# A timetable for two graph layers: in the pair attention, features are stored ahead of the pair's weights, the second layer's parts stand closer, and score rows are loaded later

## The chip, the core and the metric

The kernel runs on one core of a Trainium2 chip. The metric is the device time of one execution in microseconds. Before the change the median of three runs is 3165.02 us (3162.23 to 3175.48); the profiled execution has a span of 3169.2 us, and all times below that name a moment count from its start.

## The reference

The input is 128 graphs of 128 nodes with 256 features and a 128x128 adjacency each. Two layers follow each other. Cut to what matters:

```python
# layer 0
for W, a in ((W1, a1), (W2, a2)):             # two graph attentions
    Wh = h @ W
    e = leaky_relu(Wh @ a[:F] + swap(Wh @ a[F:]), 0.2)
    h = softmax(where(adj > 0, e, NEG), axis=1) @ Wh
h = layernorm(x + h)
x1 = layernorm(h + relu(h @ w_ff1) @ w_ff2)   # "ff0"
# layer 1: attention of 8 heads with a value matrix per relation
attn = softmax(q @ k / sqrt(32))
out = sum_r (attn * (adj == r)) @ v_r
x2 = layernorm(x1 + out @ Wo)                 # "att"
y = layernorm(x2 + gelu(x2 @ W1) @ W2)        # "ff1"
```

All of it is float32.

## The kernel before, in words

**Tiles and stages.** Four graphs make a group (`G = 4`), so there are 32 groups. Each group goes through five stages, each a Python generator: `load` (the transposed input `xt` and the adjacency `at`), `gat` (both graph attentions, `gat_block`, L428), `ff0` (the first feed forward), `att` (the attention of the second layer, `attention`, L460) and `ff1` (the second feed forward, `feed_forward`, L315). When the adjacency has no entry above 1, as here, the arm with the plan `BINARY` runs. It takes the attention of a group by pairs of graphs (`together=2`): scores of a pair (`weights`, L482), their transposition (`turned`, L511), the masks (`by_relation`), the weighted sum (`weighted`, matmuls at L557 into the tile `av`) and the output product (L584). Below, "#1" is the first pair of a group and "#2" the second.

**What sets the order.** Each `yield TIMES[...]` in a stage gives a number of units to pass before the stage goes on. In `layers` (L603) a heap holds the next moment of every stage of every group; a stage of group g starts at `period * g + begin[stage] - early`, with a period of 100 units. The work that a stage emits between two yields thus gets a place in one list, and this list is binding for two engines: for SP, the queue that issues all transfers, over the whole of the list, and for PE, the matmul engine, from moment 280 on (`kept={PE: 280, SP: 0}`):

```python
t, n, g, steps = heapq.heappop(todo)
step = next(steps, None)                  # emits the work up to the next yield
...
    if e in last and kept[e][0] <= t <= kept[e][1]:
        tc.add_manual_dep(i, last[e], ...)   # order of emission
if step is not None:
    heapq.heappush(todo, [t + step, n, g, steps])
```

The units are an order and no times. The order on DVE, ACT and POOL is chosen by the framework's scheduler, as are the PSUM banks: `mm` has 7 (`bufs`), and `av` one of its own. Five groups are in flight at a time, each in another stage.

**Transposition through memory.** A product needs its token tile with features on the partitions. `put` (L267) transposes 32x32 blocks on DVE (L282) and stores four quarters to a DRAM buffer `zd` (four stores, L285); after `yield TIMES["put"]`, `get` loads the whole back (L291). This serves `ff0`, `att` and `ff1` (tile `T`, by `features`, L296) and the attention weights of each graph (`e1` stored, `eT` loaded). `turned` stores both graphs of a pair (eight stores), waits `put`, loads the first, waits `next put`, loads the second.

**The score rows of a graph attention.** `gat_weighting` (L394) stores one row per graph to `zsd` (L405), waits `row put`, loads it to all partitions as `e` (L408), waits `row`, and then adds the column term (ACT, L411), takes the leaky maximum, the mask and the row maximum (DVE, L418 to L420), the exponential (ACT, L423), the reciprocal (L424) and the scaling (POOL, L425). After `gat` units the product with `wh` follows: L444 for the first graph attention, L455 for the second.

**The feed forward.** After `moving_sums` (POOL, L309 to L312) come eight visits, which alternate between two units of hidden features; each visit emits products at L333 and copies, sums and activations on ACT, DVE and POOL (L339 to L360). The third and fourth products of a unit write a bank that ACT copies out first (L346, L351). Then the second matrix (L378): a first half of 32 matmuls over the first unit's features, and a second half in two parts of 8 ("k0" and "k2"), each of which ends in an addition on DVE (L388).

**The pair attention.** Its list is: `features` (put, get), mask load (L242), q and k (L470, L475), scores #1 (L491), `turned` #1, values #1 (L542), masks #1 (L526), weighted sum #1 with scores #2 right behind it, output product #1 (L584, after `wo` units), `turned` #2, values #2, masks #2, weighted sum #2, output product #2. A pair's scores take four of the seven `mm` banks; each is read by a maximum on DVE (L495) and by four exponentials on ACT (L504), 16 for a pair.

Of the kernel before, what the change touches and what calls it, by code (L numbers as in the profile page):

```python
# [29 lines left out]
TIMES = {  # L30
    "sums": 5, "ff visits": (2.5, 2.5, 3, 3, 3.25, 3.25, 3.25, 3.25), "ff2": 3,
    "ff first half": 10, "ff half": 5, "row": 13, "gat": 22, "wh": 5.5,
    "gat copy": 2, "qk": 7, "scores": 18, "mask": 7, "av": 13, "wo": 8, "turned": 10,
    "put": 7, "next put": 3, "row put": 5,
    "lead ff0": 19, "lead att": 25, "lead ff1": 25, "affine": 7,
    "store": 25,
}
# [3 lines left out]
    binary=False, times=TIMES, together=1, period=560, bufs=dict(T=3, tok=2, m=4, mm=6, v=1),  # L41
    begin=dict(load=-97, gat=-61, ff0=48, att=132, ff1=400), early={},
# [1 line left out]
)  # L44

BINARY = dict(
    binary=True, times=TIMES, together=2,
    period=100, bufs=dict(T=5, tok=5, m=2, mm=7, v=2),
    begin=dict(load=-97, gat=-61, ff0=48, att=132, ff1=300),
    early={  # L50
        (1, "ff0"): 48,
        (2, "load"): 80, (2, "gat"): 80, (2, "ff0"): 80,
        (3, "load"): 5,
        (-2, "ff1"): -15,
        (-1, "load"): 5,
    },
    kept={PE: 280, SP: 0},
)
# [726 lines left out]
```

## Time and profile before

| what | value |
|---|---|
| median of three runs | 3165.02 us |
| span of the profiled execution | 3169.2 us |
| PE busy | 2816.0 us (89%) |
| ACT, POOL, DVE busy | 1682.8, 1529.4, 1510.3 us |
| mean share of the DMA engines (queue q1) | 47.3% |
| starts of L455 of one group: fourth and thirty-second | 260.39 and 2917.09 us |

A group's L455 stands at the same place of each period, so the distance of two of them is the length of a period: (2917.09 - 260.39) / 28 = 94.9 us. Idle time of an engine is put down to what released it. "SPq" is SP's queue, in which a transfer and its waits hold up all that stands behind them. PE's granted clock, in the windows view, is 1.00 at full speed.

### The profile page before, as it was taken

Reading aid. Unit: us, or ns where it says so; the run is one execution under the profiler, and the core shown is the slowest. Engines: PE = TensorE matmul, PEld = TensorE weight load, DVE = VectorE, ACT = ScalarE, POOL = GpSimd, SP = SyncE. Lnnn points to the kernel's source line nnn. Section 1 sums busy time; section 2 is a strip of 40 time slices with the busy share of each in tenths; the row PEclk is TensorE's granted clock in tenths of the full one; section 3 lists DMA queues with packets and bytes.
Section 4 is the critical chain, followed back from the end, with each engine's and each line's share of the span. In section 5 each row is a group of like instructions: output and inputs, shape, how many; then the busy total and the mean of one; then the engine's idle time right before and its main releaser. Section 6 shows DMA issues by size and latency. Waiting matters only on the chain.

```text
span 3169.2 us, 46779 instructions
## 1 busy us (share of the span) xinstructions
PE 2816.0 (89%) x16578; PEld 2173.5 (69%) x16578; DVE 1510.3 (48%) x2873; ACT 1682.8 (53%) x5063; POOL 1529.4 (48%) x1610
## 2 busy tenths in 40 slices
PE   4988989889889889889889889889889889889878
PEld 3756677667677667667667677667677667677656
DVE  5454455445445444455445445444455444445342
ACT  2455465555465554565555565555565555565443
POOL 1434455454455454555354455453555454555362
PEclk6998999999999999999999999999999999999999
DMA  6145554544543644554544553544654544543420
GB/s 262 41 90 121 122 107 89 124 88 102 125 105 90 126 97 90 127 110 90 121 91 98 125 109 86 127 98 89 127 110 86 124 89 98 127 104 80 90 50 14
DMA packets 1156947, 328.76 MB, mean 104 GB/s; under 512 B 903008, under 2 KB 1126752, under 8 KB 1156064
## 3 DMA queue, kind: packets, MB, share of 16 engines
q1 hardware_dynamic: 1156704, 325.68, 47.3%
q8 instruction: 133, 2.18, 0.3%
q14 instruction: 110, 0.90, 0.1%
HBM read 195.97 MB, written 129.62 MB: 103 GB/s over the span
## 4 chain that ended last, share of the span: by engine, by line
PE 34%; ACT 21%; POOL 18%; issue 11%; DMA 7%; SPq 5%; DVE 3%; ACTq 0%; POOLq 0%; DVEq 0%
PE mm L378 14%; ACT e L504 7%; POOL tok L265 6%; PE mm L470 5%; DMA T<-zd 5%; SPq L285 5%; POOL e L507 4%; ACT fT L354 4%; POOL rstd L256 4%; ACT tok L259 4%; PE mm L333 3%; PE mm L475 3%; PE av L557 3%; PE mm L542 3%; ACT e L423 1%
## 5 line engine op out<-in xcount | busy, mean ns | idle before, releaser
L265 POOL TENSOR_TENSOR tok<-tok,ln_rows 128x512 f32<-128x512 f32 x476 | 618.5, 1320 | 20.8 <-PE mm L276 12.8
L378 PE MATMUL mm<-w,fT 128*128 128x256 f32 x2048 | 460.7, 381 | 0.0
L378 PE MATMUL mm<-wf,fT 128*128 128x256 f32 x2048 | 456.7, 381 | 1.5 <-ACT fT L354 1.5
L378 PEld LDWEIGHTS mm<-w,fT 128*128 128x128 f32 x2048 | 386.6, 190 | 67.4 <-issue 13.9
L378 PEld LDWEIGHTS mm<-wf,fT 128*128 128x128 f32 x2048 | 386.4, 190 | 57.5 <-ACT fT L354 1.9
L507 POOL TENSOR_TENSOR e<-e,s 128x1024 f32<-128x1024 f32 x128 | 241.4, 1897 | 343.2 <-DVE s L506 269.0
L504 ACT ACTIVATE e<-mm,nm 128x128 f32<-128x128 f32 x1024 | 358.2, 394 | 46.2 <-DVE nm L495 45.8
L259 ACT ACTIVATE tok<-tok,nmr,rstd 128x256 f32<-128x256 f32 x480 | 249.1, 589 | 200.7 <-POOL nmr L257 189.3
L309 POOL TENSOR_TENSOR t<-T 128x256 f32<-128x256 f32 x64 | 50.8, 793 | 550.1 <-DMA T<-zd 550.1
L470 PE MATMUL mm<-T,wq 128*128 128x512 f32 x256 | 183.2, 881 | 137.3 <-DMA T<-zd 137.3
L425 POOL TENSOR_TENSOR e<-e,s 128x512 f32<-128x512 f32 (+1 forms) x68 | 68.1, 1002 | 430.4 <-DVE s L424 393.6
L526 DVE TENSOR_TENSOR m<-eT,am 128x1024 f32<-128x1024 f32 x128 | 176.8, 1397 | 184.0 <-DMA eT<-zd 183.5
L495 DVE TENSOR_REDUCE nm<-mm 128x4 f32<-128x512 f32 x256 | 162.3, 680 | 200.8 <-PE mm L491 200.8
L352 POOL TENSOR_TENSOR fT<-fT 128x512 f32<-128x512 f32 x128 | 161.3, 1271 | 178.3 <-ACT fT L351 178.3
L542 PE MATMUL mm<-wv,T 128*128 128x512 f32 x512 | 240.7, 615 | 0.0
L504 ACT ACTIVATION_READ_ACCUMULATOR e<-mm,nm 128x1 f32 x1024 | 240.3, 235 | 0.0
L470 PEld LDWEIGHTS mm<-T,wq 128*128 128x128 f32 x256 | 70.8, 289 | 233.9 <-DMA T<-zd 144.3
L476 ACT ACTIVATE kT<-mm,col 128x512 f32<-128x512 f32 x64 | 43.9, 687 | 326.4 <-PE mm L475 326.4
L333 PE MATMUL mm<-T,w 128*128 128x256 f32 x768 | 196.3, 384 | 0.7 <-ACT T L280 0.2
L333 PE MATMUL mm<-T,wf 128*128 128x256 f32 x768 | 192.8, 381 | 0.0
L561 ACT COPY oT<-av 128x512 f32<-128x512 f32 x64 | 37.4, 585 | 276.9 <-PE av L557 276.9
L360 ACT ACTIVATE fT<-mm,col 128x256 f32<-128x256 f32 x256 | 107.2, 472 | 137.8 <-PE mm L333 97.8
(142 smaller groups left out, 5371.6 us busy)
## 6 DMA issues: line engine op xcount, KB each, us to landing
zd<-e SPq DMA_DIRECT2D x496, 128.0 KB, 3.5
eT<-zd SPq DMA_DIRECT2D x124, 512.0 KB, 6.2
zd<-T SPq DMA_DIRECT2D x364, 128.0 KB, 3.5
T<-zd SPq DMA_DIRECT2D x91, 512.0 KB, 4.3
xt<-in_xT_dram SPq DMA_DIRECT2D x32, 512.0 KB, 5.6
e<-zsd SPq DMA_DIRECT2D x60, 256.0 KB, 4.1
tok<-in_x_dram SPq DMA_DIRECT2D x30, 512.0 KB, 4.9
out_dram<-tok SPq DMA_DIRECT2D x29, 512.0 KB, 6.0
```

The costliest lines, as they stand in the source:

```text
L259: nc.scalar.activation(y[:, b], y[:, b], AF.Identity, bias=nmr[:, b:b + 1], scale=rstd[:, b:b + 1])
L265: engine.tensor_tensor(y[:, b:b + n], y[:, b:b + n], v[:, None, :].to_broadcast([P, n, D]), op)
L285: nc.sync.dma_start(s[:, :, i].rearrange("k (j a) t -> a (k j) t", a=Q), z[ts(i, Q)].rearrange("a k (j t) -> a (k j) t", t=Q))
L333: nc.tensor.matmul(p[:, i], win[k][:, ts(f0 + i, P)], hs[k], start=first and i == 0, stop=True, skip_group_check=True)
L352: nc.gpsimd.tensor_add(hi[:, :, 1], hi[:, :, 1], hi[:, :, 0])
L378: nc.tensor.matmul(ys[b // 2][:, b % 2], fT[f][:, ts(b, N)], wout[:, f], start=b % 2 == 0 and n == 0, stop=n == FC - 1, skip_group_check=True)
L470: nc.tensor.matmul(p, c.wq[:, f, ts(i, P)], hT[:, :, f], start=f == 0, stop=f == DC - 1)
L495: nc.vector.tensor_reduce(nm.rearrange("p j i -> p (j i)"), p.rearrange("p j i n -> p (j i) n"), AX.X, OP.max, negate=True)
L504: nc.scalar.activation(e[:, k], p[:, j, i], AF.Exp, bias=nms[q][:, j, i:i + 1], accum_out=s[:, k:k + 1])
L507: nc.gpsimd.tensor_mul(e, e, per_row(s, N))
L526: nc.vector.tensor_tensor(m, eT, at[:, b][:, None, :].to_broadcast([P, H, N]), OP.mult)
L542: nc.tensor.matmul(p, hT[:, b, f], wv[:, f, r:r + 2], start=f == 0, stop=f == DC - 1)
```

## The change

Only numbers of the plan `BINARY` change. It gets times of its own for twelve of the yields, and other starts for four stages.

```diff
-    binary=True, times=TIMES, together=2,
-    period=100, bufs=dict(T=5, tok=5, m=2, mm=7, v=2),
-    begin=dict(load=-97, gat=-61, ff0=48, att=132, ff1=300),
+    binary=True, together=2, period=100, bufs=dict(T=5, tok=5, m=2, mm=7, v=2),
+    times=dict(TIMES, **{
+        "ff first half": 6, "ff half": 4, "row": 14.5, "wh": 3.5, "mask": 8.5, "av": 14.5,
+        "wo": 12, "turned": 11, "next put": 2.5, "row put": 9, "affine": 9,
+        "ff visits": (2.5, 2.5, 4, 4, 3.25, 3.25, 3.25, 3.25),
+    }),
+    begin=dict(load=-96, gat=-61, ff0=45, att=129, ff1=303),
     early={
-        (1, "ff0"): 48,
+        (1, 'ff0'): 46,
```

Before, the same entries are: ff first half 10, ff half 5, row 13, wh 5.5, mask 7, av 13, wo 8, turned 10, next put 3, row put 5, affine 7, and ff visits (2.5, 2.5, 3, 3, 3.25 four times). The other lines of `early` change their quotes only. No instruction is added or removed in a period; what changes is where the instructions stand on each engine and which bank or buffer each tile gets. What it is for: the attention's features are to be stored and loaded ahead of the weights of the pair before, the parts of the second feed-forward matrix are to stand closer together, and the score rows are to be loaded 9 units after they are stored, so that each engine finds its operands ready.

In one period (moments modulo 100) the two binding lists read, with "get" for L291 and "put" for L285:

```
SP before: att put 32, e1 #2 put 37, att get 39, eT #2 get 44 and 47, ff0 put 48, zsd 50, e 55, ff0 get 55
SP after:  att put 29, att get 36, e1 #2 put 41.5, ff0 put 45, zsd 46, eT #2 get 48.5 and 51, ff0 get 52, e 55

SP before: e1 #1 put 89, zsd 92, eT get 96, e 97, eT get 99, ff1 put 0, load 3, ff1 get 7
SP after:  e1 #1 put 86, eT get 93, zsd 93.5, eT get 95.5, e 2.5, ff1 put 3, load 4, ff1 get 10

PE before: ff0 first half 6, k0 16, av #1 + scores #2 19, k2 21, wo #1 27, L455 32, ff1 visits from 37, L436 39 and 44.5, values #2 47, ff1's last visit 57.75, q k 64, ff1 first half 64, av #2 67, scores #1 71, k0 74, wo #2 75, ff0 visits from 79, k2 79, L444 90, values #1 99
PE after:  ff0 first half 5, k0 11, k2 15, av #1 + scores #2 18.5, wo #1 30.5, L455 39, L436 39 and 42.5, ff1 visits from 40, values #2 51, q k 61, ff1's last visit 62.75, scores #1 68, ff1 first half 69, av #2 74, k0 75, ff0 visits from 76, k2 79, wo #2 86, L444 91.5, values #1 95.5
```

More of the change, by code (lines that the diff above doesn't have):

```diff
@@ L46 @@
 BINARY = dict(
-    binary=True, times=TIMES, together=2,
-    period=100, bufs=dict(T=5, tok=5, m=2, mm=7, v=2),
-    begin=dict(load=-97, gat=-61, ff0=48, att=132, ff1=300),
-    early={
-        (1, "ff0"): 48,
[L52 to L55, printed above, removed]
+    binary=True, together=2, period=100, bufs=dict(T=5, tok=5, m=2, mm=7, v=2),
[5 more added lines that the diff above has]
+    begin=dict(load=-96, gat=-61, ff0=45, att=129, ff1=303),
+    early={
+        (1, 'ff0'): 46,
+        (2, 'load'): 80,
+        (2, 'gat'): 80,
+        (2, 'ff0'): 80,
+        (3, 'load'): 5,
+        (-2, 'ff1'): -15,
+        (-1, 'load'): 5,
     },
```

## The prediction

> **What bounds the kernel now.** I read the page first, then PE's waits, the timeline of one period for PE, SP and ACT, and the windows view for the clock. The page says that PE carries the span (89% busy, the next engine 53%), so time is won only where PE idles or runs slowly.
>
> ```profile
> PE 2816.0 (89%) x16578; PEld 2173.5 (69%) x16578; DVE 1510.3 (48%) x2873; ACT 1682.8 (53%) x5063; POOL 1529.4 (48%) x1610
> ...
> PE mm L470 <- DMA T<-zd: 137.3, 28, 6.3
> PE mm L333 <- ACT fT L351: 92.3, 43, 3.4
> ...
> PE mm L333 <- ACT fT L339: 10.2, 13, 0.8
> PE mm L333 <- POOL t L309: 10.1, 11, 2.8
> ```
>
> The last four lines are PE's waits (total us, times, longest). The q product waits for the attention's features 28 times, once a period; the feed forward's seventh visit waits for an ACT copy. A wait costs more than its length:
>
> ```profile
> 1516.96 6.40 PE L470 MATMUL mm<-T,wq 128*128 128x512 f32 x8 [5.86 <-DMA T<-zd]
> ...
> 3035.98 3.60 PE L470 MATMUL mm<-T,wq 128*128 128x512 f32 x8
> ...
> 1514.00:1520.00 6.00, 3.04 (x4) 1.50 (x5) 0.00 (x0) 0.00 (x0) 0.00 (x0) 0.63 1.05 285
> 1520.00:1526.00 6.00, 6.00 (x12) 2.49 (x12) 3.68 (x4) 0.69 (x1) 0.00 (x0) 0.80 0.81 130
> ```
>
> The same eight records take 6.40 us after the wait and 3.60 us in the last group, where there is none; in the windows (the number before the last two is the granted clock) the clock falls to 0.63 and 0.80 behind the wait. Why it waits is seen in SP's queue:
>
> ```profile
> 1501.09 2.67 SPq L285 DMA_DIRECT2D zd<-T  x4
> 1503.86 7.32 SPq L285 DMA_DIRECT2D zd<-e  x8
> 1511.23 1.86 SPq L291 DMA_DIRECT2D T<-zd  x1
> ```
>
> The features are stored at 1501 to 1504, but their load stands behind the pair's eight stores and is issued at 1511 to 1513; q starts at 1516.96.
>
> **What the Trainium skill says.** "TensorE: Matmul & The Clock Gate", Part 1 (the HAM clock gate): the clock is halved after an idle window of about 3.4 us and restored after a busy one. The trace agrees: half clock after the 4 to 6 us waits, none after most of 2 us. "DMA: Bandwidth & Descriptors", "Two DMAs through the same engine are not ordered": a load of bytes that another transfer writes must wait for that transfer's completion semaphore. So the load cannot follow its stores directly; in the trace the ff0 load is issued 3.2 us after the last ff0 store was issued (1521.49, 1524.69). "Perfetto Trace Analysis", "Tensor Engine Instruction": ACT, DVE and GPSIMD are strictly first in, first out; so what stands early on them holds what is behind, as SP's queue does here.
>
> **Part 1: features ahead of the pair.** SP's order becomes att put, att get, e1 #2 put. ff0's k2 also moves ahead of av #1 and scores #2 on PE, and DVE's addition L388 then stands before the scores' maxima; before, it stood behind a reciprocal that waits for exponentials (k2 ended at 1583.2, its L388 ran at 1586.22). Count from the end of scores #2 (1579.6 before). Before: transposed at +18.0, load landed and q at +33.5 (1613.11). After: exponentials done at about +7.4, then the normalisation (L259, 2.1), DVE L282 (1.25): +10.8; stores 2.7: +13.5; completion 2.6 to 3.2: +16.4; landing 4.3 (page): +20.7. PE reaches q after wo, L455, L436 (twice), six visits and values #2, by durations of the timeline 1.75 + 1.75 + 3.5 + 8.7 + 3.5 + 0.9 = 20, plus the stall of part 3: about +23. So q does not wait: 137.3 us go, and with it the half clock: L470 is busy 183.2 us on the page against 32 x 3.60 = 115.2, so 68 us.
>
> **Part 2: waits on L351.** In ff0, wo #2 (1.75 us) now stands before the fifth visit and L444 (1.75 us) between the fifth and the sixth; in ff1, q and k (6.9 us) stand before the last visit. ACT needs about 4 us of copies and activations before L351 and, in ff0, one normalisation instead of two ahead of it. I get PE's seventh visit of ff0 at 5.2 us after the fourth, and L351 done 4.9 after it: hidden, with nothing to spare. I take 72 of the 92.3 us as gone, and the 10.1 us on POOL L309, since L436 now fills that place.
>
> **Part 3: the added wait, scores' banks.** Before, between scores #2 and the first matmul that takes one of its four banks stand k2, wo and half of L455; after, k2 has moved ahead, and wo (1.75) and L455 (1.75) alone remain. Built, L436's first product takes the bank of the first score tile, which is free after ten of the sixteen exponentials.
>
> ```profile
> 1578.45 1.17 PE L491 MATMUL mm<-kT,T 32*128 32x128 f32 x32
> 1579.56 3.72 PE L378 MATMUL mm<-wf,fT 128*128 128x256 f32 x16
> 1583.12 1.89 PE L584 MATMUL mm<-wo,oT 128*128 128x256 f32 x8
> 1584.84 1.89 PE L455 MATMUL mm<-wh,e 128*128 128x256 f32 x8
> ...
> 1580.37 0.37 ACT L504 ACTIVATE e<-mm,nm 128x128 f32<-128x128 f32 x1 [1.19 <-DVE nm L495]
> ...
> 1583.47 0.41 ACT L504 ACTIVATE e<-mm,nm 128x128 f32<-128x128 f32 x1
> ```
>
> In the ACT lines the tenth exponential starts at 1583.47: ready at +4.3. DVE now has L431 (0.99 us) between the first and second maximum, which sets the second tile's exponentials back by about 1 us: +5.3. L436 would start at +3.5. So it stalls 1.9 us (0.9 if L431 costs nothing; 4.4 if L431 also waits for its adjacency load, which now is issued some 5 us before the scores' end). Behind L436 on PE stands all else. 28 x 1.9 = 53 us. It is under the length after which the clock fell.
>
> **Part 4: eT #2 later.** Its loads now stand behind the ff0 features' stores and zsd, and DVE's masks (L526) stand ahead of the maxima of scores #1. Chain from +10.8: e1 #2 stores end at +24.5 (7.4 after the features' load and the mask), ff0's four stores at +28.5, eT issued +29.5, landed +36 to +37 (6.2, page), masks +38.2, maxima and 16 exponentials +44.4, then on ACT L411, L423, the copy L561 and L339: +50.8. PE comes to the third ff0 visit, which needs L339, at +50.9, and to av #2 at +39.4. It just fits; I put 0.7 us a period as the mean, 20 us, with 0 and 4 us as ends.
>
> **Part 5: at no cost.** The rows loaded 9 units on: e #2 now stands behind both eT loads and lands some 4 us before ACT would hold the copy that wo #1 needs. The 1.5 to 4 units on mask, av, next put and affine move DVE and POOL work within slack (48% busy). Loads of xt and at move by one unit behind ff1's stores. Start and end, where few groups are in flight, I take as unchanged.
>
> **Sum.** 137 + 68 + 72 + 10 - 53 - 20 = 214 us: 3165 - 214 = 2951. A check from the other side: a period has 86.7 us of busy PE (mean of six in the windows view), less 2.8 of slow clock (6.42 against 3.60 for L470) = 83.9; with 1.9 + 0.7 and some 0.8 of waits left it is 87.3 against 94.9, x 28 = 213.
>
> **Rivals.**
> (a) All hidden: banks come free earlier and eT in time. 137 + 68 + 92 + 10 - 28 x 0.9 = 282: about 2883. For it: DVE and ACT are half idle. Against it: the banks' order as built. 0.13.
> (b) The bank stall is long (L431 waits for its load): 4.4 us x 28 = 123, and the clock falls with it, 1.7 us x 28 = 48. 137 + 68 + 72 + 10 - 123 - 48 - 20 = 96: about 3069. For it: the adjacency load moves nearer to its use. 0.14.
> (c) eT #2 lands 3 us late (1.8 MB of stores and loads stand ahead): 84 us in place of 20: 287 - 53 - 84 = 150: about 3015. 0.15.
> (d) Slower: e #2, behind two eT loads of 512 KB and the token load, lands over 10 us late; ACT is first in, first out, so oT, wo #1 and the exponentials all wait some 8 us, the bank stall follows and the clock falls. 1.9 + 8 + 2.4 = 12.3 x 28 = 344 against 287: about 3220. Against it: the trace's e loads were used within 7 us. 0.10.
> My own case has 0.48.
>
> **How the numbers follow.** The likeliest is 2951. From 2870 (case a with no stall at all is 2858) to 3080 (case b and its margin) only (d) and the extremes are left out. Faster: all but (d) and a little of (b), 0.87; same 0.03; slower 0.10.
>
> **What would show it.** Right: no wait of L470 on T<-zd, L470 busy near 115 us, clock 1.00 in nearly all windows, periods of 86 to 88 us; a new wait of L436 on ACT L504 or DVE L431 of about 2 us. Wrong: the q wait stays (features stored later than +13.5), PE waits at av #2, at L333 on L339 or at wo #1 on oT, or the clock is halved at the new stall.

## The result and the profile after

The changed kernel takes **2834.11 us** (median of four, 2832.35 to 2836.63); the kernel before, run beside it, takes 3163.62 us (3161.88 to 3175.48). The ratio is 0.8952, with a 95% interval of 0.8929 to 0.8975. The direction was as forecast; the time lies 117 us under the 2951 and 36 us under the lower end of the range. All line numbers of the changed kernel are those of before plus 6: L470 is now L476, L351 is L357, L339 is L345, L436 is L442.

The page of the changed kernel, PE's busy time and the granted clock in 40 slices of the span:

```profile
PE 2718.5 (96%) x16578; PEld 2148.2 (76%) x16578; DVE 1527.5 (54%) x2873; ACT 1679.3 (59%) x5063; POOL 1547.0 (55%) x1610
...
PEclk7898999999999999999999999999999999999999
```

The same 16578 matmuls are busy for 97.5 us less, and the span shrank from 3169.2 to 2831.9 us, by 337.3. So idle time of PE fell by 337.3 - 97.5 = 239.8 us. Both halves have to be explained. First the idle part, from PE's waits in the changed kernel (total us, times, longest); these two are all that is left in the steady state:

```profile
PE mm L339 <- ACT fT L345: 10.5, 13, 1.8
...
PE mm L339 <- ACT fT L357: 2.7, 7, 0.8
```

The wait of q on its features (137.3 us) is gone, the one behind L351 (now L357) fell from 92.3 to 2.7 us, and the one on L339 (now L345) stayed, 10.2 against 10.5. The forecast bank stall is not in the list: L442 never waits for an exponential or a cap. One period of PE, from scores #2 to ff0's third visit:

```profile
1336.49 1.17 PE L497 MATMUL mm<-kT,T 32*128 32x128 f32 x32
...
1341.15 1.92 PE L442 MATMUL mm<-wx,xt 128*128 128x260 f32 x8
...
1359.89 3.60 PE L476 MATMUL mm<-T,wq 128*128 128x512 f32 x8
...
1388.27 1.03 PE L339 MATMUL mm<-t,wf1s 128*128 128x256 f32 x4
```

Scores #2 end at 1337.66. L442 starts 3.5 us later, right behind wo and L461; q starts 22.2 us later and takes 3.60 us; the third ff0 visit starts 50.6 us later. None has an idle time in brackets. ACT in the same period, the fourth exponential of the pair (the first starts at 1338.40) and the copy L345 on which the third ff0 visit depends:

```profile
1339.45 0.37 ACT L510 ACTIVATE e<-mm,nm 128x128 f32<-128x128 f32 x1
...
1387.13 0.58 ACT L345 COPY fT<-mm 128x512 f32<-128x512 f32 x1
```

The first bank of scores is read by these first four exponentials and is free at 1339.8, 1.3 us ahead of L442. L345 ends at 1387.71, 0.56 us ahead of the visit that needs it. SP's queue shows the features' stores, their load, and eT #2:

```profile
1347.70 2.66 SPq L291 DMA_DIRECT2D zd<-T  x4
1353.11 0.38 SPq L297 DMA_DIRECT2D T<-zd  x1
...
1366.80 1.46 SPq L297 DMA_DIRECT2D eT<-zd  x2
```

The load follows 15.5 us after the scores' end with nothing between it and the stores but their completion, and has landed when q comes. The windows view of this period (PE's busy time first, the granted clock third from the end):

```profile
1339.42:1422.53 83.11, 82.77 (x514) 65.81 (x512) 46.04 (x89) 52.33 (x160) 49.23 (x52) 1.00 0.57 121
```

The clock is full and PE is idle for 0.3 us. From L461 to the same L461 28 groups on, 254.16 to 2591.14, a period is 83.46 us against 94.88 before: 28 x 11.42 = 319.7 us. The start is 6.2 us shorter and what follows the last L461 is 11.4 us shorter, together 337.3.

The busy part, from the groups by line of the kernel before (busy us, mean ns, then idle time ahead of them):

```profile
L542 PE MATMUL mm<-wv,T 128*128 128x512 f32 x512 | 240.7, 615 | 0.0
...
L333 PE MATMUL mm<-t,wf 128*128 128x256 f32 x256 | 74.2, 415 | 70.0 <-ACT fT L351 70.0
```

L470 went from 183.2 to 115.1 us, as foreseen. But these two groups, which follow the waits on L351, also went down, to 230.2 and 65.7 us. Two values products of before, each 1 us behind a wait of 2.17 us on L351, show why:

```profile
801.84 5.29 PE L542 MATMUL mm<-wv,T 128*128 128x512 f32 x8
...
1561.82 3.60 PE L542 MATMUL mm<-wv,T 128*128 128x512 f32 x8
```

The first was slow (granted clock 0.56 from 803 to 806), the second was not. Of 28 waits of 2.2 to 2.6 us ahead of a values product 8 were followed by a slow one, of 4.1 to 5.3 us. In the changed kernel all take 3.60 us. I had priced the slow clock for L470 only. Not all of the drop is the clock behind L351: 1.4 of L542's 10.5 us lie in the last group, behind waits on POOL, and of the 8.5 us of the second group about 2.9 are no clock: the four records right behind a wait take 1.13 us against 1.03 at full clock too, 29 times (an estimate from the timeline).

### The profile page after: what moved, and what is told of

The parts are those of the page before. It is cut to its first block, busy times and chain, and to the rows that moved or that the text cites. A ratio compares the mean times of both kernels' runs of the same rounds, so it can differ in the third digit from the quotient of the medians.

```text
span 2831.9 us, 46682 instructions
## 1 busy us (share of the span) xinstructions
PE 2718.5 (96%) x16578; PEld 2148.2 (76%) x16578; DVE 1527.5 (54%) x2873; ACT 1679.3 (59%) x5063; POOL 1547.0 (55%) x1610
## 4 chain that ended last, share of the span: by engine, by line
PE 62%; ACT 11%; DVE 10%; DMA 6%; POOL 5%; issue 4%; SPq 1%; ACTq 0%; DVEq 0%; POOLq 0%
PE mm L384 23%; PE mm L339 16%; PE mm L548 4%; PE mm L476 4%; DMA eT<-zd 4%; PE mm L481 4%; ACT e L510 3%; PE av L563 3%; ACT fT L360 2%; PE mm L590 2%; DVE nm L501 2%; ACT tok L265 2%; PE mm L497 2%; POOL e L513 2%; PE mm L450 2%
## 5 line engine op out<-in xcount | busy, mean ns | idle before, releaser
L384 PE MATMUL mm<-wf,fT 128*128 128x256 f32 x2048 | 448.7, 379 | 1.5 <-ACT fT L360 1.5
L513 POOL TENSOR_TENSOR e<-e,s 128x1024 f32<-128x1024 f32 x128 | 254.4, 1994 | 133.7 <-DVE s L512 118.4
L429 ACT ACTIVATE e<-e,nm 128x128 f32<-128x128 f32 x256 | 99.6, 390 | 298.3 <-DVE nm L426 292.0
L510 ACT ACTIVATION_READ_ACCUMULATOR e<-mm,nm 128x1 f32 x1024 | 247.8, 242 | 0.0
L548 PE MATMUL mm<-wv,T 128*128 128x512 f32 x512 | 230.2, 592 | 0.0
L339 PE MATMUL mm<-T,wf 128*128 128x256 f32 x768 | 197.4, 381 | 0.0
L339 PE MATMUL mm<-T,w 128*128 128x256 f32 x768 | 194.4, 382 | 0.3 <-ACT T L286 0.2
L360 ACT ACTIVATE fT<-fT,col 128x512 f32<-128x512 f32 x256 | 167.8, 711 | 29.9 <-DVE fT L354 29.4
L256 DVE BATCH_NORM_STATS2 st<-tok 128x6 f32<-128x256 f32 x480 | 179.8, 412 | 4.1
L394 DVE TENSOR_TENSOR tok<-tok,mm 128x512 f32<-128x512 f32 x120 | 81.8, 681 | 182.7 <-PE mm L384 182.7
L339 PEld LDWEIGHTS mm<-T,w 128*128 128x128 f32 x768 | 147.1, 192 | 35.6 <-issue 15.5
L548 PEld LDWEIGHTS mm<-wv,T 128*128 128x128 f32 x512 | 97.1, 190 | 95.1 <-issue 87.5
```

Source lines behind the costliest of these rows:

```text
L256: nc.vector.bn_stats(st, y[:, b])
L339: nc.tensor.matmul(p[:, i], win[k][:, ts(f0 + i, P)], hs[k], start=first and i == 0, stop=True, skip_group_check=True)
L360: nc.scalar.activation(lo[:, i], lo[:, i], func, bias=bin_[:, f0 + i:f0 + i + 1])
L384: nc.tensor.matmul(ys[b // 2][:, b % 2], fT[f][:, ts(b, N)], wout[:, f], start=b % 2 == 0 and n == 0, stop=n == FC - 1, skip_group_check=True)
L510: nc.scalar.activation(e[:, k], p[:, j, i], AF.Exp, bias=nms[q][:, j, i:i + 1], accum_out=s[:, k:k + 1])
L513: nc.gpsimd.tensor_mul(e, e, per_row(s, N))
```

## The experiments

The first five runs start from the kernel before and add parts of the change; the other seven start from the changed kernel and take one thing back. Each ratio is to the kernel before run beside it.

**1. The queue alone (`e1_queue_alone`).** The second pair's stores are emitted 3 units later, so that SP's order is features, load, pair; PE's list is unchanged.

```diff
-                yield TIMES["turned"]
-                eT = yield from turned(es)
+                yield TIMES["turned"] + 3
+                eT = yield from turned(es, TIMES["put"] - 3)
```

> The timetable of before with one move: the second pair's eight stores are emitted 3 units later, so that SP's queue holds the attention's features load ahead of them; PE's list is that of before. Theory (queue order is the cause of the q wait): features' load issued about 5.3 us after its first store and landed 4.3 us later, which is before PE comes to q; the q wait (137 us) and its half clock (68 us) go; eT of the second pair comes some 4 us later and takes back 1 to 2 us a period: 2960 to 3010. The waits on L351 (92 us) stay. Rival (the gain needs the new order on PE, since features are ready too late): q still waits, 3100 to 3164.

Measured: 3149.27 us, ratio 0.9941 (0.9921 to 0.9961). The q product no longer waits and takes 3.60 us, yet almost nothing is won. PE's waits show where it went, and ACT's timeline why:

```profile
PE mm L333 <- ACT e L504: 114.8, 27, 4.5
```

```profile
1527.21 1.28 ACT L411 ACTIVATE e<-e,wh 128x128 f32<-128x128 f32 x4 [10.74 <-DMA e<-zsd]
```

The wait on q had covered another lateness. With it gone, PE ends scores #1 (at 1525.64) before ACT has had the score rows, whose L411 and L423 stand ahead of the pair's exponentials; these start at 1533.59, so the banks of the scores come free late. The slow clock moved along with the wait: L470 is busy 67.7 us less than before, and PE as a whole 8.6 us more (2824.6 against 2816.0). The 137 us were moved to the next wait, not won. My range was missed by 140 us.

**2. The queue and ACT's order (`e10_queue_rows`).** The score rows' steps come 4 units later as well, and the following product keeps its place, so on ACT L423 falls behind the exponentials.

```diff
-        yield TIMES["row"]
+        yield TIMES["row"] + 4
...
-        yield TIMES["gat"]
+        yield TIMES["gat"] - 4
```

> The first experiment (timetable of before, features' load ahead of the pair's stores) with one more move: a graph attention's arithmetic is emitted 4 units later and its product 4 units less after it, so that PE's and SP's lists stay as they were and ACT holds the row exponentials (L423) behind the pair's (L504), not ahead of them. Theory (in the first experiment the q wait came back as a wait for a score bank, because ACT had the late score rows' work in front of the pair's exponentials): exponentials start some 4 us earlier, the bank wait (115 us) and its half clock go, L351's 100 us stay: 2970 to 3015. Rival (the period is held by the features' chain anyway, the wait only moves on): 3100 to 3150.

Measured: 3070.43 us, ratio 0.9694 (0.9666 to 0.9722). The wait on the exponentials fell from 114.8 to 22.7 us and the time by 79 us. The wait on L351, 100.4 us in run 1, rose to 110.8 us, and 26.7 us on L340 are new; the time stays 55 us short of my range. A part of the lateness moved once more.

**3. And the feed forward's spacing (`f3_rows_ff`).**

```diff
-    "ff first half": 10, "ff half": 5, "ff visits": (2.5, 2.5, 3, 3, ...
+    "ff first half": 6, "ff half": 4, "ff visits": (2.5, 2.5, 4, 4, ...
```

> The kernel before with the pair's second stores 3 units later and the score rows 4 units later (as in the run of 3070 us), and now also with the feed forward's two parts 6/4 units apart and its third and fourth visits 4 units, as in the changed kernel. SP's order is unchanged by it. ff0's k2 stays behind scores #2 on PE, but ff1's k2 is wholly ahead of the first visits. In ff0 two normalisations still stand ahead of L351 on ACT. Theory A (the waits on L351 come from the two normalisations ahead of it on ACT): they stay, 90 us or more, and the time is 3030 to 3080. Theory B (they come from the parts being too close to the visits on PE): the waits fall under 50 us and the time to 2960 to 3010.

Measured: 2997.07 us, ratio 0.9464 (0.9433 to 0.9494). The time is that of theory B, the waits on L351 (85.8 us) nearly those of theory A; neither was right as it stood. By tile, 66.1 of the 85.8 us are in ff0 (70.0 before) and 19.7 in ff1 (22.3 before), and 32.8 us on L339 are new in ff0. The periods are not alike. In about half of them ff0 waits 3.4 to 4.1 us on L351, in the others 1.8 to 2.9 us on L339 and 1.2 us on L351. ACT and then PE of one ff0 of the first kind:

```profile
1478.88 2.08 ACT L259 ACTIVATE tok<-tok,nmr,rstd 128x256 f32<-128x256 f32 x4 [2.62 <-POOL nmr L257]
```

```profile
1487.45 2.08 PE L333 MATMUL mm<-t,wf 128*128 128x256 f32 x4 [4.02 <-ACT fT L351]
```

Two normalisations stand ahead of L354 and L351 on ACT (the second at 1481.33), 4.1 us together, about as long as the wait. In the period before it (1380 to 1400) the first of them stands ahead of a copy L339, and PE waits 2.49 us there.

**4 and 5. Where wo #2 stands (`f5_wo_late`, `f6_wo_both`).** Both start from run 3. In the first, wo #2 comes 6 units later, and both normalisations stay ahead of L351. In the second, both wo come 4 units later, wo #2 thus 8, and one normalisation falls behind L351. My texts ahead of the runs place wo #2 one visit too late: in the traces it stands between ff0's first and second visits in the first run, and between the second and third in the second.

```diff
-            yield TIMES["wo"]
+            yield TIMES["wo"] + (6 if b else 0)     # f5_wo_late
+            yield TIMES["wo"] + 4                   # f6_wo_both
```

> The kernel of the run of 2997 us (q's queue, the score rows and the feed forward's spacing changed, L351 waiting 85.8 us, about 4 us in each ff0) with wo #2 6 units later: on PE between ff0's second and third visits. On ACT both normalisations of ff0's time still stand ahead of L354 and L351. Theory A (ACT's two normalisations make L351 late): the wait stays near 4 us a period less at most the 1.75 us of wo: 50 to 90 us, 2960 to 3000. Theory B (PE comes to the seventh visit too soon, and every product put between the visits takes its length off): 28 x 1.75 = 49 us go, with the slow clock behind them: 2920 to 2955.

> The kernel of the run of 2997 us with both wo 4 units later, as in the changed kernel: wo #2 stands between ff0's third and fourth visits, and on ACT one of the two normalisations now stands behind L351; on SP ff0's stores come before the two eT loads, as in the changed kernel. Theory A (the two normalisations): L351's waits fall under 25 us and the time to 2870 to 2920, against 2834 for the whole change. Theory B (spacing on PE alone): as the run with wo #2 alone, 2920 to 2955.

Measured: 3052.23 us, ratio 0.9639 (0.9613 to 0.9664), and 2936.44 us, ratio 0.9274 (0.9249 to 0.93). Two ff0 of `f6_wo_both` on PE:

```profile
1455.53 1.13 PE L333 MATMUL mm<-t,wf 128*128 128x256 f32 x4 [2.66 <-ACT fT L351]
...
1540.70 1.13 PE L333 MATMUL mm<-t,wf 128*128 128x256 f32 x4 [0.79 <-ACT fT L351]
```

In `f5_wo_late` ff0's waits on L351 doubled, from 66.1 to 132.8 us (those on L339 in ff0 went), and the time rose by 55 us, past both theories: with two normalisations ahead, a product between the first visits did not hide the wait. In `f6_wo_both`, with one normalisation moved behind L351, ff0's waits on L351 and L339 fell together from 98.9 to 43.2 us: 0.8 us in half of the periods and 2.1 to 2.7 us in the others, where the one normalisation that is left comes 1.5 us later after the fourth visit. So ACT's order is the likelier cause for ff0; no run moves a normalisation alone. Theory A's sums were missed all the same, 71.0 us of waits where it had under 25 and 16 us of time, since ff1 has 27.8 us of them here, 19.7 in run 3.

The ladder is then: 3149, 3070, 2997, 2936 us, and 2834 with the whole timetable. No rung holds the gain. The 71.0 us of waits on L351 that the last rung still has, against 2.7 with the whole change, are most of its remaining 102 us; PE is also busy 30.8 us longer (2749.3 against 2718.5).

**6. The queue undone (`e2_queue_undone`).** From here on the base is the changed kernel. Its pair stores #2 go ahead of the features' load again; PE's list stays.

```diff
-                yield TIMES["turned"]
-                eT = yield from turned(es)
+                yield TIMES["turned"] + -6
+                eT = yield from turned(es, TIMES["put"] - -6)
```

> The new timetable with one move undone: the second pair's stores stand ahead of the attention's features load on SP again; PE's list is the new one. Theory: the load is issued about 21 us after the scores' end instead of 15.5 and lands at 25, PE comes to q at 22: a q wait of about 3 us a period, 85 us, with little or some half clock: 2920 to 2965. Rival (the earlier k2 on PE does it all): 2834 within 10.

Measured: 2971.08 us, ratio 0.9383 (0.9363 to 0.9403).

```profile
PE mm L476 <- DMA T<-zd: 89.6, 28, 4.2
```

The wait is as expected, 3.2 us a period; the time went up by 137 us, a little over the range. Nearly all of the 47 us beyond the wait are q's slow clock: L476 is busy 160.5 us against 115.1 in the changed kernel, and the mean clock is 0.964 against 0.982. Here, with all else in order, SP's order is worth its wait and the slow clock behind it in full.

**7. The score rows undone (`e11_rows_undone`).** The rows are loaded 5 units after their store and used 13 units later, as before; on ACT, L417 then stands between the two copies of k.

```diff
-        ... "row": 14.5, ... "row put": 9,
+        ... "row": 13, "gat": 27.5, ... "row put": 5,
```

> The new timetable with the score rows' part undone: rows loaded 5 units after the store and used 13 later (9 and 14.5 in the new one), and the product 5.5 units later behind them, so that PE's list stays the new one. On SP the rows' load moves one place, ahead of the second eT load; on ACT the rows' L411 now stands between the two copies of k. Theory (ACT's place of the rows' work is what the 9 units buy): rows land about 8 us after k's copy is due, the second copy waits behind them, PE waits for it before the scores: 8 us and 2 us of half clock a period, 3060 to 3130. Rival (the load's place in the queue alone matters): 2834 to 2870.

Measured: 3093.32 us, ratio 0.9758 (0.9728 to 0.9787), as expected. PE's list is that of the changed kernel, and yet 259 us are lost, the most of any run that takes one thing back. ACT's timeline:

```profile
1586.41 1.28 ACT L417 ACTIVATE e<-e,wh 128x128 f32<-128x128 f32 x4 [7.23 <-DMA e<-zsd]
1587.59 0.67 ACT L482 ACTIVATE kT<-mm,col 128x512 f32<-128x512 f32 x1
```

The rows' load is issued at 1581.59, behind an eT load; ACT waits for it, the second copy of k stands behind, and scores #1 on PE wait for that copy 200.9 us in all, up to 8.6 us at a time. This is the queueing that the Trainium skill states in "Perfetto Trace Analysis", "Tensor Engine Instruction": ACT takes its instructions strictly in order, and the trace agrees. The rest of the loss lies in PE's busy time, 72.2 us longer (2790.7 against 2718.5), nearly all of it in scores #1 and the second matrix behind them.

**8. The visits' spacing undone (`f1_visits_undone`).**

```diff
-        "ff visits": (2.5, 2.5, 4, 4, 3.25, 3.25, 3.25, 3.25),
+        "ff visits": (2.5, 2.5, 3, 3, 3.25, 3.25, 3.25, 3.25),
```

> The changed kernel with the third and fourth visits of the feed forward 3 units apart again instead of 4. SP's order is that of the changed kernel; on ACT the score rows' L417 now stands ahead of the exponentials of scores #1, and one normalisation ahead of those of scores #2. Theory A (ACT's order is what the spacing is for): the rows' load is issued about 1 us after the scores' end and takes 3.2 us, so the exponentials start some 4 us later once a period and PE's first taker of a score bank waits 2 to 4 us, 28 times: 2890 to 2950, with waits on ACT e L510. Theory B (the spacing is of no weight; only SP's order and the places of the products count): 2825 to 2850, without such waits.

Measured: 2901.9 us, ratio 0.9171 (0.9147 to 0.9195). Theory A's range held, though the weight lay in the other half of its edit: not the rows ahead of scores #1, but the normalisation ahead of the exponentials of scores #2. This run shows the bank stall that I had forecast for the change. PE, and the fourth exponential on ACT:

```profile
1379.47 1.14 PE L442 MATMUL mm<-wx,xt 128*128 128x260 f32 x4 [1.81 <-ACT e L510]
```

```profile
1378.97 0.35 ACT L510 ACTIVATE e<-mm,nm 128x128 f32<-128x128 f32 x1
```

The exponentials start at 1377.94, behind a normalisation of 2.07 us. The fourth ends at 1379.32, and L442 starts 0.15 us later. So a bank needs four exponentials, not ten, and the stall comes only where ACT begins late: 56.5 us over the run.

**9. The order of the exponentials (`e3_exp_by_graph`).** The 16 exponentials are chained in the source's order, graph by graph, so that the first bank would be free after ten.

```diff
+                        if prev is not None:
+                            tc.add_manual_dep(it, prev, ...)
+                        prev = it.name
```

> The new timetable with the 16 exponentials of a pair forced into the order of the source on ACT, all of the first graph ahead of the second, so that the first score bank is free after ten of them and not after four. Theory A (my bank stall did not come because ACT takes the exponentials tile by tile): L436's first product waits about 1 us a period, 2850 to 2880. Theory B (the framework gives that product whichever bank it holds to be free first, so a stall does not come with either order): 2834 within 10, and no wait of PE on the exponentials.

Measured: 2870.3 us, ratio 0.9067 (0.905 to 0.9085). Apart from one wait of 1.8 us near the start no product waits for an exponential: the banks went to other tiles, so the stall could not be tried in this way. The 28 short waits of L442's weight loads, 7.2 us in all, now end with DVE's L597, which reads the output product. What grew is the other close place:

```profile
PE mm L339 <- ACT fT L357: 25.4, 27, 1.5
```

together with 17.5 us on L345. The time lies in theory A's range, but by chance, as its wait is missing. The run shows how little slack ACT's chain has, and is inconclusive on Part 3; run 8 decides that.

**10. k2 behind scores #2 (`e4_k2_behind`).**

```diff
-        yield TIMES["ff first half"]
+        yield 10 if before == "01" else TIMES["ff first half"]
...
-            yield TIMES["ff half"]
+            yield 5 if before == "01" else TIMES["ff half"]
```

> The new timetable, but ff0's second-matrix part k2 stands behind the first pair's weighted sum and scores again (first half 10 and half 5 units in ff0 alone); SP's order is the new one. Theory (k2 ahead makes the features about 7 us earlier): features' stores begin at +16 to +18 after the scores' end in place of +10, landed at +26 to +28, q on PE at +25.7: a wait of 0.5 to 2 us a period, 2850 to 2890. Rival (k2's place is of no matter, as SP's order alone gives the time): 2834 within 10.

Measured: 2936.57 us, ratio 0.927 (0.9244 to 0.9296), 47 us over the range. The wait on q's features is 19.0 us (21 times, up to 2.2), as expected. What I had not seen are 54.5 us on L345. Later features push the pair's stores, eT #2, its masks and exponentials and so L345: in the period at 1471.83 the loads of eT #2 are issued 37.1 us after the scores' end, against 29.1 in the changed kernel. This is the chain of Part 4, which has half a microsecond of slack.

**11. eT #2 ahead of ff0's stores (`e8_pair_loads_first`).** It was meant to give that chain more slack.

```diff
-    begin=dict(load=-96, gat=-61, ff0=45, att=129, ff1=303),
+    begin=dict(load=-96, gat=-61, ff0=51.5, att=129, ff1=303),
...
-        yield TIMES["lead ff0" if before == "01" else "lead ff1"]
+        yield TIMES["lead ff0"] - 6.5 if before == "01" else TIMES["lead ff1"]
```

> The new timetable with ff0's features stored and loaded 6.5 units later, so that the second pair's eT loads stand ahead of these stores on SP; PE's list is the new one. Theory (the wait on L339 that is left, 10.5 us, hangs on eT of the second pair): eT lands about 3 us earlier, that wait goes: 2820 to 2830. Rival (ff0's features come too late for its first visits, or the rest of the time is PE's own): 2834 or more.

Measured: 2887.67 us, ratio 0.9132 (0.9099 to 0.9165). The waits on L345 fell from 10.5 to 1.9 us, as meant, but scores #1 now wait 37.7 us for q's copy, and the waits on L357 rose from 2.7 to 12.0 us. DVE:

```profile
1478.95 1.23 DVE L532 TENSOR_TENSOR m<-eT,am 128x1024 f32<-128x1024 f32 x1 [4.66 <-DMA eT<-zd]
1480.09 0.75 DVE L477 TENSOR_SCALAR T<-mm,col 128x512 f32<-128x512 f32 x1
```

A mask that waits for eT now stands between the two copies of q. In the changed kernel both copies are ahead of it.

**12. wo #2 earlier (`e7_wo2_early`).**

```diff
-            yield TIMES["wo"]
+            yield TIMES["wo"] - (4 if b else 0)
```

> The new timetable with the second pair's output product 4 units earlier, between ff0's third and fourth visits, no longer between the fourth and fifth. Theory (that product on PE covers ACT's work up to L351): the seventh visit comes 1.75 us sooner after the fourth, its slack in the trace is about 1 us, so a wait of 0.7 us a period on L351: 2845 to 2860. Rival (L351 was late before because of the two normalisations ahead of it on ACT, not for want of cover on PE): 2834 within 5.

Measured: 2834.45 us, ratio 0.8949 (0.8926 to 0.8972): no difference. L357's waits stay small (4.5 us), so the rival's forecast held. But ACT's order did not stay: the one normalisation that stands ahead of L357 in ff0 of the changed kernel comes after it here. The cover on PE went and the work ahead of L357 on ACT went with it, so the run does not test the place of the product alone. That the wait stays away without the cover agrees with runs 4 and 5.

## Why the prediction was wrong in size

Step by step, predicted gain against what the two traces show:

| step | predicted | shown |
|---|---|---|
| Part 1, wait of q | 137 | 137.3 |
| Part 1, half clock of L470 | 68 | 68.1 (183.2 to 115.1) |
| Part 2, waits on L351 | 72 | 89.6 (92.3 to 2.7) |
| Part 2, slow records behind waits | not priced | 19.0 (L542 10.5, L333 t,wf 8.5) |
| wait on POOL L309 | 10 | 7.3 |
| Part 3, bank stall | -53 | 0 |
| Part 4, eT #2 and L339 | -20 | -0.3 |
| rest, start and end among it | 0 | 16.3 |
| sum | 214 | 337.3 between the two spans |

**Part 1 was right** in mechanism and size for the whole change: 15.5 us to the load's issue where I had 16.4, q at 22.2 where I had 23. The second figure was partly luck: it holds the stall of Part 3, which did not come, and counts 8.7 us for six visits, whose 12 products took 10.4. My durations alone make 20, which would have been ahead of the features' landing, put at 20.7. What I had not seen is that it holds only together with the rest: alone it gave 0.6% (run 1), because the wait had covered the late score rows.

**Part 2 was mis-sized.** The waits were hidden almost wholly. I had named that one normalisation leaves ACT's list ahead of L351, but counted it as leaving "nothing to spare": PE's seventh visit came 5.2 us after the fourth, as I had it, and L351 (now L357) was done 4.15 us after it and not 4.9. And I took the slow clock only where a single record showed it doubled. The windows view had it: my check counted 83.9 us of busy PE a period, after taking off L470's surplus alone, and the changed kernel needs about 82.9.

**Part 3 failed at its premise**, "free after ten of the sixteen exponentials". I took the order of the loops in the source for the order on ACT. Built, the exponentials run bank by bank; the first bank is free after four, 2.2 us after the scores' end, and L442 comes at 3.5. The cap took 0.42 us, not 0.99. Run 8 shows both the four and the stall when ACT starts late. The order could have been read from the trace before: by the semaphores that the packed trace keeps, the first, fifth, ninth and thirteenth exponential wait for a maximum of DVE, in the kernel before and in the changed one.

**Part 4's chain was right** to within a microsecond: +50.8 predicted for L339's end, +50.05 measured, against +50.9 and +50.6 for PE's arrival, which rests on the same +23. The term put on it failed: I charged 0.7 us a period for a close fit, where the waits stayed as they had been before, 10 us in 13 periods. That it is close is shown by runs 9 and 10.

**Part 5 was right** that the new places of the rows cost nothing, but blind to what they are for: with the rows' old load and use times in the new timetable 259 us are lost (run 7). It was wrong that start and end stay as they were. They are 6.2 and 11.4 us shorter, which is about the whole of the rest in the table; why was not taken apart.

**The case that came** is rival (a), everything hidden, which I gave 0.13 at 2883; with the stall set to nothing in it I had written 2858, and the slow records behind waits (19 us) and the rest (16.3 us) more than cover the 24 us from there to the result. Rivals (b) to (d) did not occur.

## What to carry to other kernels

When one wait is removed in an engine-bound pipeline, look at once for the next thing that would be late at that place; the full gain appears only when every in-order list (SP's queue, ACT, DVE) is put in the order in which its operands arrive, and a single such list left as it was can take most of it back. Read the order of instructions on each engine as built, never from the loops of the source, before a bank or buffer is said to be held. Where a wait slows the clock, price all records behind it by their mean duration against their fastest, not only the first. And read more than one period: in runs 3 and 5 the waits alternate from period to period.

## What the runs showed of the hardware that I had not expected

In these traces waits of 4 us slowed also what came 2 us later: in run 4 (`f5_wo_late`) the values product behind a 4.04 us wait took 4.23 us, and in run 3 it took 5.67 us behind 4.02 us, against 3.60 us undisturbed. Repeated waits of up to 2.3 and 2.9 us (L442 in run 8, L497 in run 11) left the mean clock at 0.980 and 0.978, close to the 0.982 of the changed kernel. Yet a short wait is not always free: in the kernel before, the clock fell behind 8 of 28 waits of 2.2 to 2.6 us, all shorter than the 3.4 us that the prediction goes by, and two waits of 2.17 us were followed by 5.29 and by 3.60 us. What tells them apart was not found. And in runs 1 and 8 a matmul that waited for a bank started about 0.15 us after the last read of it ended.
